# An FP32 cross-attention kernel: a third form made on GpSimd, another order of work in the steady batches, and new durations in the planner

## The chip, the cores and the metric

The kernel runs on one core of one Trainium2 chip. The metric is the device time of one execution in microseconds (us), taken as the median of several runs. TensorE is called PE in the profile, its weight loads PEld, VectorE DVE, ScalarE ACT, GpSimd POOL and SyncE SP; a `q` behind a name means the engine's queue, which issues transfers.

## The reference, cut to what matters

There are 32 batches; x and y (`ctx_2048`) are 32 x 256 x 1024 in float32, the weights 256 x 256.

```python
B, C, N = (8, 256, 1024)          # B is 32 in the inputs
x_q = jnp.einsum('oc,bcn->bno', w_qk, y)
x_k = jnp.einsum('oc,bcn->bon', w_qk, x)
x_v = jnp.einsum('oc,bcn->bon', w_v, x) + b_v[None, :, None]
energy = jnp.einsum('bnc,bcm->bnm', x_q, x_k)
attention = jax.nn.softmax(energy, axis=-1)
attention = attention / (1e-07 + attention.sum(axis=1, keepdims=True))
x_r = jnp.einsum('bcn,bnm->bcm', x_v, attention)
x_r = jax.nn.relu(jnp.einsum('oc,bcn->bon', w_t, x - x_r) + b_t[None, :, None])
return x + x_r
```

## The kernel before, in words

**Forms.** The operands of PE are tiles of type float32r. Each operand is split into three forms: for x, y and ef these are HIGH (the value written as float32r), REST (the value less HIGH) and LOW (HIGH/4096 + REST); gf, uf and the weights have variants of them. A product is a sum of three float32r products, taken in the order HIGH, REST, LOW. The two query and key weight matrices are multiplied together once, in the set-up (`gw`), and w_t is multiplied into w_v (`vw`), so each batch has five kinds of product, all of 128 x 128 weights by 512 columns:

- `k0`, `k1` (`keys`): gw times x gives gf, a pair of PSUM banks for each, 12 matmuls for each. ACT and DVE then make gf's three forms from the banks.
- `V0`, `V1` (or `v0`, `v1`; `values`): x times vw, 12 matmuls each. DVE transposes blocks into the tile `turned`, SP writes it to DRAM in four transfers (`blocks<-turned`) and reads it back: the first half into `yr` (`yr<-blocks`), the second into `turned`. From there ACT and POOL make the three forms `uf`.
- `W0`, `W1` (`straight`): x times tw, 12 matmuls each, which ACT copies with a bias into `xe`.
- `E0` to `E7` (`energy`): 128 rows of y times gf, 12 matmuls, two banks of 512 columns (h0, then h1). Then the softmax of these rows: DVE takes the minimum, ACT the exponential with its sum, DVE the reciprocal; for each half DVE adds the scaled row to `acc`, ACT makes HIGH of `ef`, DVE makes REST; ACT makes LOW and POOL adds REST to LOW. The pair of banks is free again after the last REST.
- `A0` to `A7` (`attention`): uf times ef, 12 matmuls into pairs 2 and 3, where all eight add up.

Then `S` (`sums`) sums `acc` down the columns on DVE, and `O` (`finish`) scales the attention result, adds `xe`, applies relu, adds x (`xo`) and stores. `Y2` and `Y3` (`load_y`) load the two halves of the next batch's y, `X` (`load_x`) the next batch's x.

**PSUM.** Of four pairs of banks, pairs 0 and 1 alternate among `E`, `k` and `v`; a unit marked `^` takes pair 3 or 2 in turn, while attention does not hold them.

**Buffers.** There is one raw buffer `yr` (128 x 1024 float32, 512 KB) for y's halves, which the read-back `yr<-blocks` also uses; two buffers `yf` of y's forms, one for each half of the rows (E0 to E3 read the first, E4 to E7 the second); four buffers `ef`.

**Order.** The strings SET_UP, FIRST (batch 0), STEADY (batches 1 to 29), BEFORE (batch 30) and LAST (batch 31) list units; PE does them exactly in that order. All the rest is ordered by a planner (`Plan`): each unit adds its operations with an assumed engine duration (`busy`), a time until others see the result (`lag`, for transfers the landing), and the names it reads and writes. The planner works out due times and runs a list schedule over the whole program; what comes out of it is each engine's fixed instruction order, and ties go to the operation that was listed first. The engines then run their queues strictly in order. SP issues loads, read-backs and stores; POOL issues the adding transfers.

**y's forms before.** In `load_y`, SP loads `yr`, ACT copies it to HIGH. ACT then writes -HIGH into the third form, and a transfer that POOL issues adds y itself from DRAM onto it (`yf<-in_ctx_dram`), which gives REST. ACT writes HIGH/4096 into LOW and a second adding transfer (`yf<-yf`) adds REST. In the set-up alone, y's first half is cut in two pieces of 256 columns, and the first piece's REST and LOW are made on POOL by `tensor_tensor`; the second piece is read by E2 and E3.

Of the kernel before, what the change touches and what calls it, by code (L numbers as in the profile page):

```python
# [16 lines left out]
class Plan:  # L17
# [146 lines left out]

SET_UP = (
    "z z x0 z z z z G H fH00 x1 fH01 T fR01 fL00 y fR00 fL01 Q fR11 fH10 fR10 fL10 b fH11 fL11"
)
# [1 line left out]
    "V0^ W0^ W1^ E0 E1^ V1^ E2 E3 A0 A1 E4 X Y2 E5 A2 A3 E6 E7 A4 Y3 A5 v0 k0 S A6 A7 k1 O"  # L171
)
STEADY = (
    "W0^ E0^ E1 E2 W1^ V1^ E3 Y2 A0 E4 A1 E5 A2 X E6 A3 E7 Y3 S A4 A5 v0 k1 A6 A7 k0 O"
)
BEFORE = (
    "V1^ E0 W0^ E1 W1^ X E2 A0 E3 A1 E4 A2 E5 A3 E6 E7 Y2 A4 Y3 A5 v0 k0 k1 A6 S A7 O"
# [7 lines left out]
def kernel(  # L185
# [55 lines left out]
        plan.add("pe", count * (columns / 2400 + 1 / 400), 0.163, reads, writes, trace)  # L241

    def on_act(columns, reads, writes, trace, more=0.0):
        plan.add("act", columns / 1200 + 0.1 + more, 0.09, reads, writes, trace)

    def on_dve(columns, reads, writes, trace, early=0.0):
        plan.add("dve", columns / 960 + 0.16, 0.0, reads, writes, trace, early=early)

    def dve_in_sbuf(columns, reads, writes, trace):
        busy = columns / 960 + 0.07  # L250
# [3 lines left out]
        plan.add("dve", busy, 0.0, reads, writes, trace)  # L254

    def on_pool(columns, reads, writes, trace):
        busy = columns * 2.25 / 1024 + 0.12
        plan.add("pool", busy, 0.0, reads, writes, trace, port=busy)

    def by_sync(landing, reads, writes, trace, early=0.0):  # L260
        plan.add("sync", 0.4, landing, reads, writes, trace, early=early)
# [7 lines left out]
    def value(v):  # L269
        return v.bitcast(F32)  # L270
# [7 lines left out]
    def parted(v):  # L278
        return v.rearrange("p (a b) -> p a b", a=2)
# [60 lines left out]
    def load_y(q):  # L340
        b, half = divmod(q, MH)
        s = q % NY
        f, r = yf[s], yr
        from_ = y[b].rearrange("(k p) n -> p k n", p=P)[:, :, ts(half, MB)]
        by_sync(5.8 if q else 7.4, [], ["yr"], lambda: sync.dma_start(r, from_), early=0.0 if q else 10.0)
        on_act(N, ["yr"], y_names(s, HIGH), lambda: act.copy(f[:, HIGH], r))

        def pieces(which):
            at = slice(which[0] * QB, (which[-1] + 1) * QB)
            high, low, third = (f[:, j, :, at] for j in range(FORMS))  # L350
            nh, nl, nr = (y_names(s, j, which) for j in range(FORMS))
            columns = KC * QB * len(which)
            if q == 0 and which[0] == 0:
                on_pool(
                    columns, ["yr"] + nh, nr,
                    lambda: pool.tensor_tensor(third, r[:, :, at], value(high), ALU.subtract),
                )
                on_act(columns, nh, nl, lambda: act.mul(low, value(high), 1.0 / UP))
                on_pool(columns, nl + nr, nl, lambda: pool.tensor_tensor(low, value(low), value(third), ALU.add))
                return  # L360
            on_act(columns, nh, nr, lambda: act.mul(third, value(high), -1.0))
            by_pool(7.2, nr, nr, lambda: accumulate(third, from_[:, :, at]))
            on_act(columns, nh, nl, lambda: act.mul(low, value(high), 1.0 / UP))
            by_pool(5.8, nl + nr, nl, lambda: accumulate(value(low), value(third)))

        for which in ([0], [1]) if q == 0 else ([0, 1],):
            pieces(which)
# [4 lines left out]
    def load_x(b):  # L372
        for k in range(KC):

            def of(k=k):
                raw = [f"xr{k}{h}" for h in range(MH)]
                by_sync(5.0, ["yr"] if b == 1 else [], raw, lambda: sync.dma_start(xr[:, k], x[b, ts(k, P)]))
                on_act(N, raw, x_names(HIGH, k), lambda: act.copy(parted(xf[:, HIGH, k]), in_turn(xr[:, k])))
                on_pool(
                    N, raw + x_names(HIGH, k), x_names(REST, k),  # L380
                    lambda: pool.tensor_tensor(
                        parted(xf[:, REST, k]), in_turn(xr[:, k]), parted(value(xf[:, HIGH, k])), ALU.subtract
                    ),
                )
                on_act(
                    N, x_names(HIGH, k), x_names(LOW, k),
                    lambda: act.mul(xf[:, LOW, k], value(xf[:, HIGH, k]), 1.0 / UP),
                )
                by_pool(
                    8.2, x_names(LOW, k) + x_names(REST, k), x_names(LOW, k),  # L390
                    lambda: accumulate(value(xf[:, LOW, k]), value(xf[:, REST, k])),
                )

            of()
# [41 lines left out]
    def values(b, q, j_pair):  # L436

        both, at, u = pair(j_pair), in_pair(j_pair), uf[q]
        for i in range(KC):
            for j in ORDER:  # L440

                def of(i=i, j=j):
                    for k in range(KC):
                        matmul(
                            both[:, i], vw[:, j, k, ts(i, P)], woven(xf[:, j, k], q),
                            j == ORDER[0] and k == 0, j == ORDER[-1] and k == KC - 1,
                        )

                on_pe(KC, MB, [f"vw{j}{k}" for k in range(KC)] + [f"xf{j}{k}{q}" for k in range(KC)], [at[i]], of)
        on_dve(  # L450
            N, at, ["turned"],
            lambda: dve.transpose(
                turned.rearrange("p (a t i r) -> p i t a r", a=NG, t=HT, i=KC),
                both.rearrange("p i (t a r) -> p i t a r", t=HT, a=NG),
            ),
        )
        names = [f"uf{q}{j}" for j in range(FORMS)]

        def out_of():
            for g in range(NG):  # L460
                sync.dma_start(
                    blocks.rearrange("(a r) (g s) -> r g a s", a=NG, g=NG)[:, g],
                    turned[ts(g, G32)].rearrange("p (a s) -> p a s", a=NG),
                )

        plan.add("sync", 2.4, 3.0 if b else 5.0, ["turned"], ["blocks"], out_of)
        back, name = (turned, "turned") if q else (flat(yr), "yr")
        by_sync(4.5, ["blocks"], [name], lambda: sync.dma_start(back, blocks))

        def natural(v):  # L470
            return v.rearrange("p (t g s) -> p g t s", t=HT, g=NG)

        raw = back.rearrange("p (g t s) -> p g t s", t=HT, g=NG)
        high, low, rest = (natural(u[:, j]) for j in range(FORMS))
        on_act(N, [name], [names[HIGH]], lambda: act.copy(high, raw))
        on_pool(
            N, [name, names[HIGH]], [names[LOW]],
            lambda: pool.tensor_tensor(low, raw, value(high), ALU.subtract),
        )
        on_act(N, [names[LOW]], [names[LOW]], lambda: act.mul(u[:, LOW], value(u[:, LOW]), UP))  # L480
        on_pool(
            N, [name, names[LOW]], [names[REST]],
            lambda: pool.tensor_tensor(rest, raw, value(low), ALU.subtract),
        )
# [9 lines left out]
    def energy(b, n, jp):  # L494
# [6 lines left out]
        for j, h in steps:  # L501
# [13 lines left out]
        on_dve(N, at, [nm[0]], lambda: dve.tensor_reduce(low, p, AX.X, ALU.min))  # L515
        on_act(
            N, at + [nm[0]], at + [nm[1]],
            lambda: act.activation(p, p, AF.Exp, bias=low, scale=-1.0, accum_out=rs), more=0.193,
        )
        dve_small(0.18, [nm[1]], [nm[2]], lambda: dve.reciprocal(ri, rs))  # L520

        def halves(h):
            ph, a, turns = both[:, h], acc[:, ts(h, MB)], in_turn(both[:, h])
            to = {j: parted_half(f[:, j], h) for j in (HIGH, REST)}
            high, rest = names[HIGH][h], names[REST][h]
            if n == 0:
                on_dve(MB, [at[h], nm[2]], [f"acc{h}"], lambda: dve.tensor_scalar(a, ph, ri, None, ALU.mult))
            else:
                on_dve(
                    MB, [at[h], nm[2], f"acc{h}"], [f"acc{h}"],  # L530
                    lambda: dve.scalar_tensor_tensor(a, ph, ri, a, ALU.mult, ALU.add),
                )
            on_act(MB, [at[h], nm[2]], [high], lambda: act.mul(to[HIGH], turns, ri))
            on_dve(
                MB, [at[h], nm[2], high], [rest],
                lambda: dve.scalar_tensor_tensor(
                    to[REST], turns, ri, value(to[HIGH]), ALU.mult, ALU.subtract
                ),
            )

        for h in range(MH):
            halves(h)
        on_act(N, names[HIGH], names[LOW], lambda: act.mul(f[:, LOW], value(f[:, HIGH]), 1.0 / UP))
        on_pool(
            N, names[LOW] + names[REST], names[LOW],
# [229 lines left out]
    def first_x(k):  # L775
        for h in range(MH):

            def of(h=h):
                at = ts(h, MB)
                high, low, rest = (parted_half(xf[:, j, k], h) for j in range(FORMS))  # L780
                raw, (nh, nl, nr) = in_turn(xr[:, k, at]), (x_names(j, k, (h,)) for j in range(FORMS))
                on_act(MB, [f"xr{k}{h}"], nh, lambda: act.copy(high, raw))
                dve_in_sbuf(MB, [f"xr{k}{h}"] + nh, nr, lambda: dve.tensor_tensor(rest, raw, value(high), ALU.subtract))
                dve_in_sbuf(
                    MB, nh + nr, nl,
# [181 lines left out]
```

## Time and profile before

| | |
|---|---|
| median of 3 runs | 1881.93 us (1878.26 to 1883.33) |
| the profiled execution, its own time | 1882.61 us |
| its span, first to last instruction | 1880.7 us |
| mean granted TensorE clock | 0.998 |
| busy, of the span | PE 1855.6 us (99%), PEld 1597.4, POOL 1541.4 (82%), DVE 1493.0 (79%), ACT 1484.8 (79%) |
| DMA | 301.88 MB, of which 99.10 MB from POOL's queue |

How to read it: matmuls overlap one another, so PE's busy time counts their modelled lengths; the rate at which they start is what tells the time. A row of the timeline has its start, its length, the engine, the operation, the tile written and those read, the count of instructions that were merged, and in brackets the idle time before it with what ended that. A row of the windows gives, for a stretch of time, the busy time and the count of each engine, then the granted clock (PEclk), the DMA engines' busy share and their rate.

### The profile page before, as it was taken

The page shows a single profiled execution, that of the slowest core. Times are in us where ns is not written, and L with a number is a line of the kernel's source. Part 1 is how long each engine was busy: PE and PEld are TensorE (multiplying, and loading weights), DVE is VectorE, ACT ScalarE, POOL GpSimd, SP SyncE. Part 2 cuts the span into 40 slices and gives each one's busy share as a digit, 9 for nine tenths or more (in the row PEclk, how much of TensorE's full clock was granted, in tenths as well). Part 3 has the DMA queues.
Part 4 walks back from the last instruction along what each step waited for, and adds up shares of the span by engine and source line. Part 5 has one row for each costly group of instructions (what it writes and reads, how often), then busy time and mean ns, then how long its engine had stood idle before and what let it go on. Part 6 is the DMA issues. An engine that isn't in the chain of part 4 may idle for free.

```text
span 1880.7 us, 24352 instructions
## 1 busy us (share of the span) xinstructions
PE 1855.6 (99%) x8494; PEld 1597.4 (85%) x8494; DVE 1493.0 (79%) x2106; ACT 1484.8 (79%) x1936; POOL 1541.4 (82%) x773
## 2 busy tenths in 40 slices
PE   8999999999999999999999999999999999999998
PEld 7888888888888888888888888888888888888887
DVE  6787777887778878878777787777887877877878
ACT  6788777897777987778877789777797777887775
POOL 4788888888788888788888888888888788888777
PEclk9999999999999999999999999999999999999999
DMA  6666766667667667666676666666767666667652
GB/s 187 137 154 169 178 157 157 162 163 178 160 154 170 154 183 173 152 153 162 167 180 157 157 160 165 175 160 152 174 152 184 169 154 151 170 165 177 150 119 79
DMA packets 128651, 301.88 MB, mean 161 GB/s; under 512 B 12688, under 2 KB 47120, under 8 KB 128528
## 3 DMA queue, kind: packets, MB, share of 16 engines
q1 hardware_dynamic: 92272, 200.45, 34.4%
q0 software_dynamic: 35680, 99.10, 31.0%
q8 instruction: 66, 1.08, 0.2%
q10 hardware_dynamic: 576, 0.79, 0.1%
q14 instruction: 57, 0.47, 0.1%
HBM read 167.38 MB, written 67.11 MB: 125 GB/s over the span
## 4 chain that ended last, share of the span: by engine, by line
PE 33%; ACT 28%; DVE 14%; DMA 11%; issue 8%; POOL 4%; SPq 1%; DVEq 0%; POOLq 0%; ACTq 0%
PE banks L231 33%; ACT ef L231 10%; DMA blocks<-turned 6%; ACT banks L231 5%; DVE ef L231 5%; ACT xf L231 5%; DMA yr<-blocks 4%; DVE acc L231 4%; ACT xe L231 3%; ACT uf L231 3%; POOL ef L231 2%; DVE small L231 2%; ACT z L231 1%; SPq L231 1%; DVE parts L231 1%
## 5 line engine op out<-in xcount | busy, mean ns | idle before, releaser
L231 PE MATMUL banks<-gf,yf 128*128 128x512 f32 x3072 | 705.5, 381 | 8.5 <-DMA yf<-yf 2.8
L231 POOL TENSOR_TENSOR ef<-ef 128x1024 fp32r<-128x1024 f32 x256 | 640.5, 2516 | 79.8 <-DVE acc L231 35.4
L231 PE MATMUL banks<-ef,uf 128*128 128x512 f32 x3072 | 694.7, 379 | 1.1 <-POOL ef L231 0.6
L231 PEld LDWEIGHTS banks<-gf,yf 128*128 128x128 f32 x3072 | 576.2, 189 | 107.5 <-DVE ef L231 24.9
L231 PEld LDWEIGHTS banks<-ef,uf 128*128 128x128 f32 x3072 | 580.2, 189 | 85.1 <-POOL ef L231 1.4
L231 DVE TENSOR_REDUCE small<-banks 128x1 f32<-128x1024 f32 x256 | 312.5, 1221 | 174.1 <-PE banks L231 174.1
L231 DVE SCALAR_TENSOR_TENSOR ef<-banks,small,ef 128x512 fp32r<-128x512 f32 x512 | 366.5, 742 | 48.5 <-ACT ef L231 47.6
L231 ACT ACTIVATE ef<-banks,small 128x512 fp32r<-128x512 f32 x512 | 335.5, 706 | 4.1 <-DVE acc L231 0.6
L231 DVE SCALAR_TENSOR_TENSOR acc<-banks,small,acc 128x512 f32<-128x512 f32 x448 | 319.6, 743 | 5.7
L231 ACT ACTIVATE banks<-banks,small 128x1024 f32<-128x1024 f32 x256 | 281.8, 1101 | 23.2 <-DVE small L231 23.0
L231 ACT ACTIVATE ef<-ef 128x1024 fp32r<-128x1024 f32 x256 | 276.7, 1081 | 1.2
L231 ACT ACTIVATE gf<-banks 128x1024 fp32r<-128x1024 f32 x64 | 65.4, 1023 | 261.7 <-PE banks L231 259.8
L231 POOL TENSOR_TENSOR z<-z,xe 128x1024 f32<-128x1024 f32 (+1 forms) x64 | 149.1, 2345 | 68.2 <-DVE z L231 65.7
L231 POOL TENSOR_TENSOR uf<-yr,uf 128x1024 fp32r<-128x1024 f32 x64 | 152.2, 2377 | 57.4 <-ACT uf L231 57.1
L231 PE MATMUL banks<-xf,vw 128*128 128x512 f32 x768 | 183.4, 383 | 7.5 <-DVE ef L231 6.7
L231 PE MATMUL banks<-xf,gw 128*128 128x512 f32 x768 | 177.3, 380 | 1.1 <-DVE xf L231 0.7
L231 PE MATMUL banks<-xf,tw 128*128 128x512 f32 x774 | 176.5, 378 | 0.9 <-DVE banks L231 0.9
L231 PEld LDWEIGHTS banks<-xf,vw 128*128 128x128 f32 x768 | 142.6, 189 | 38.2 <-DVE ef L231 19.2
L231 PEld LDWEIGHTS banks<-xf,gw 128*128 128x128 f32 x768 | 144.7, 189 | 23.5 <-ACT acc L231 1.1
L231 PEld LDWEIGHTS banks<-xf,tw 128*128 128x128 f32 x774 | 145.4, 189 | 22.1 <-DVE banks L231 1.3
L231 POOL TENSOR_TENSOR uf<-turned,uf 128x1024 fp32r<-128x1024 f32 x64 | 154.9, 2420 | 8.5 <-ACT uf L231 6.2
L231 POOL TENSOR_TENSOR xf<-xr,xf 128x1024 fp32r<-128x1024 f32 x62 | 149.3, 2429 | 1.0 <-ACT xf L231 1.0
(68 smaller groups left out, 1633.8 us busy)
## 6 DMA issues: line engine op xcount, KB each, us to landing
yr<-in_ctx_dram SPq DMA_DIRECT2D x64, 512.0 KB, 4.3
blocks<-turned SPq DMA_DIRECT2D x256, 128.0 KB, 3.2
yf<-in_ctx_dram POOLq DMA_DIRECT2D x63, 512.0 KB, 6.1
yf<-yf POOLq DMA_DIRECT2D x63, 512.0 KB, 7.4
xo<-in_x_dram SPq DMA_DIRECT2D x62, 512.0 KB, 4.4
xr<-in_x_dram SPq DMA_DIRECT2D x62, 512.0 KB, 4.8
xf<-xf POOLq DMA_DIRECT2D x62, 512.0 KB, 6.7
out_dram<-z SPq DMA_DIRECT2D x62, 512.0 KB, 4.1
```

Of the source, the lines that this page charges most:

```text
L231: self.last = getattr(self.engine, name)(*args, **kwargs)
```

## The change

1. In `load_y`, the third form is made by POOL as a difference, yr - HIGH, in one `tensor_tensor`. ACT's multiplication by -1 and the adding transfer from DRAM are gone. `yr` is then read by POOL too.
2. STEADY has a new order. On PE it differs in one place: `E3 A0 E4 A1 E5 A2 E6 A3 E7` becomes `E3 A0 A1 E4 E5 A2 A3 E6 E7`. The units without PE work `Y2`, `X`, `S` and `O` stand elsewhere in the list.
3. The planner's durations change: ACT, DVE and POOL operations, ACT's copies of x (+0.47 us, +0.26 in the set-up), the exponential, and the landings of transfers. They alter no instruction, only the order in which instructions are queued.
4. The softmax's pieces are listed as both column sums, both HIGH, both REST, with the switches SUMS, HIGHS, RESTS all at 2 (two halves each, as before).

```diff
+SUMS, HIGHS, RESTS = 2, 2, 2
+LAND_Y, LAND_X, LAND_BLOCKS, LAND_BACK, LAND_LOW = 4.8, 4.5, 2, 5.2, 5
...
 STEADY = (
-    "W0^ E0^ E1 E2 W1^ V1^ E3 Y2 A0 E4 A1 E5 A2 X E6 A3 E7 Y3 S A4 A5 v0 k1 A6 A7 k0 O"
+    "W0^ E0^ E1 E2 W1^ V1^ E3 A0 A1 E4 E5 A2 A3 E6 Y2 X E7 Y3 A4 A5 v0 k1 A6 A7 S O k0"
 )
...
     def on_act(columns, reads, writes, trace, more=0.0):
-        plan.add("act", columns / 1200 + 0.1 + more, 0.09, reads, writes, trace)
+        plan.add("act", columns / 1200 + 0.13 + more, 0.1, reads, writes, trace)
     def on_dve(columns, reads, writes, trace, early=0.0):
-        plan.add("dve", columns / 960 + 0.16, 0.0, reads, writes, trace, early=early)
+        busy = columns / 960 + (0.08 if columns > MB else 0.13)
+        plan.add("dve", busy, 0.08, reads, writes, trace, early=early)
...
     def on_pool(columns, reads, writes, trace):
-        busy = columns * 2.25 / 1024 + 0.12
-        plan.add("pool", busy, 0.0, reads, writes, trace, port=busy)
+        busy = columns * 2.25 / 1024 + 0.07
+        plan.add("pool", busy, 0.08, reads, writes, trace, port=busy)
...
-        by_sync(5.8 if q else 7.4, [], ["yr"], lambda: sync.dma_start(r, from_), early=0.0 if q else 10.0)
+        by_sync(LAND_Y if q else 7.4, [], ["yr"], lambda: sync.dma_start(r, from_), early=0.0 if q else 10.0)
...
-            on_act(columns, nh, nr, lambda: act.mul(third, value(high), -1.0))
-            by_pool(7.2, nr, nr, lambda: accumulate(third, from_[:, :, at]))
+            on_pool(
+                columns, ["yr"] + nh, nr,
+                lambda: pool.tensor_tensor(third, r[:, :, at], value(high), ALU.subtract),
+            )
             on_act(columns, nh, nl, lambda: act.mul(low, value(high), 1.0 / UP))
-            by_pool(5.8, nl + nr, nl, lambda: accumulate(value(low), value(third)))
+            by_pool(LAND_LOW, nl + nr, nl, lambda: accumulate(value(low), value(third)))
...
-                by_sync(5.0, ["yr"] if b == 1 else [], raw, lambda: sync.dma_start(xr[:, k], x[b, ts(k, P)]))
-                on_act(N, raw, x_names(HIGH, k), lambda: act.copy(parted(xf[:, HIGH, k]), in_turn(xr[:, k])))
+                by_sync(LAND_X, ["yr"] if b == 1 else [], raw, lambda: sync.dma_start(xr[:, k], x[b, ts(k, P)]))
+                on_act(
+                    N, raw, x_names(HIGH, k), lambda: act.copy(parted(xf[:, HIGH, k]), in_turn(xr[:, k])), more=0.47
+                )
...
-                    8.2, x_names(LOW, k) + x_names(REST, k), x_names(LOW, k),
+                    LAND_LOW, x_names(LOW, k) + x_names(REST, k), x_names(LOW, k),
...
-        plan.add("sync", 2.4, 3.0 if b else 5.0, ["turned"], ["blocks"], out_of)
+        plan.add("sync", 1.75, LAND_BLOCKS if b else 5.0, ["turned"], ["blocks"], out_of)
-        by_sync(4.5, ["blocks"], [name], lambda: sync.dma_start(back, blocks))
+        by_sync(LAND_BACK, ["blocks"], [name], lambda: sync.dma_start(back, blocks))
...
-            lambda: act.activation(p, p, AF.Exp, bias=low, scale=-1.0, accum_out=rs), more=0.193,
+            lambda: act.activation(p, p, AF.Exp, bias=low, scale=-1.0, accum_out=rs), more=0.1,
...
-        for h in range(MH):
-            halves(h)
+        each, whole = [[h] for h in range(MH)], [list(range(MH))]
+        for make, pieces in ((column_sums, SUMS), (high_form, HIGHS), (rest_form, RESTS)):
+            for hs in each if pieces == MH else whole:
+                make(hs)
```

More of the change, by code (lines that the diff above doesn't have):

```diff
@@ L517, in energy, with part @@
             N, at + [nm[0]], at + [nm[1]],
-            lambda: act.activation(p, p, AF.Exp, bias=low, scale=-1.0, accum_out=rs), more=0.193,
+            lambda: act.activation(p, p, AF.Exp, bias=low, scale=-1.0, accum_out=rs), more=0.1,
         )
         dve_small(0.18, [nm[1]], [nm[2]], lambda: dve.reciprocal(ri, rs))
[L522 to L525, printed above, removed]
+        def part(t, hs):
+            return t[:, hs[0] * MB : (hs[-1] + 1) * MB]
@@ L526, in halves, with column_sums @@
+        def column_sums(hs):
+            ph, a = part(p, hs), part(acc, hs)
+            banks_, sums_ = [at[h] for h in hs], [f"acc{h}" for h in hs]
             if n == 0:
-                on_dve(MB, [at[h], nm[2]], [f"acc{h}"], lambda: dve.tensor_scalar(a, ph, ri, None, ALU.mult))
+                on_dve(
+                    MB * len(hs), banks_ + [nm[2]], sums_,
+                    lambda: dve.tensor_scalar(a, ph, ri, None, ALU.mult),
+                )
             else:
                 on_dve(
-                    MB, [at[h], nm[2], f"acc{h}"], [f"acc{h}"],
+                    MB * len(hs), banks_ + [nm[2]] + sums_, sums_,
@@ L531, in halves, with turned_to, high_form @@
                     lambda: dve.scalar_tensor_tensor(a, ph, ri, a, ALU.mult, ALU.add),
                 )
-            on_act(MB, [at[h], nm[2]], [high], lambda: act.mul(to[HIGH], turns, ri))
+        def turned_to(j, hs):
+            return parted(f[:, j])[:, :, hs[0] * MB // 2 : (hs[-1] + 1) * MB // 2]
+        def high_form(hs):
+            turns = in_turn(part(p, hs))
+            on_act(
+                MB * len(hs), [at[h] for h in hs] + [nm[2]], [names[HIGH][h] for h in hs],
+                lambda: act.mul(turned_to(HIGH, hs), turns, ri),
+            )
@@ L534, in halves, with rest_form @@
+        def rest_form(hs):
+            turns = in_turn(part(p, hs))
             on_dve(
-                MB, [at[h], nm[2], high], [rest],
+                MB * len(hs), [at[h] for h in hs] + [nm[2]] + [names[HIGH][h] for h in hs],
+                [names[REST][h] for h in hs],
                 lambda: dve.scalar_tensor_tensor(
-                    to[REST], turns, ri, value(to[HIGH]), ALU.mult, ALU.subtract
+                    turned_to(REST, hs), turns, ri, value(turned_to(HIGH, hs)), ALU.mult, ALU.subtract
@@ L781, in of @@
                 raw, (nh, nl, nr) = in_turn(xr[:, k, at]), (x_names(j, k, (h,)) for j in range(FORMS))
-                on_act(MB, [f"xr{k}{h}"], nh, lambda: act.copy(high, raw))
+                on_act(MB, [f"xr{k}{h}"], nh, lambda: act.copy(high, raw), more=0.26)
                 dve_in_sbuf(MB, [f"xr{k}{h}"] + nh, nr, lambda: dve.tensor_tensor(rest, raw, value(high), ALU.subtract))
```

## The prediction

> **What bounds the kernel now.** I read the page's line of busy times first, then the windows, the waits, and the timeline at the places where PE waits.
>
> ```profile
> PE 1855.6 (99%) x8494; PEld 1597.4 (85%) x8494; DVE 1493.0 (79%) x2106; ACT 1484.8 (79%) x1936; POOL 1541.4 (82%) x773
> 147.48:1767.24 1619.76, 1610.76 (x7394) 1390.09 (x7392) 1294.52 (x1821) 1295.64 (x1680) 1353.45 (x673) 1.00 0.68 164
> 957.79:1015.35 57.56, 57.43 (x266) 49.66 (x265) 46.18 (x66) 46.34 (x60) 48.36 (x25) 1.00 0.68 162
> 947.43 5.34 PE L231 MATMUL banks<-ef,uf 128*128 128x512 f32 x24
> 952.61 2.75 PE L231 MATMUL banks<-xf,gw 128*128 128x512 f32 x12
> ```
>
> PE is the bound: 24 matmuls take 952.61 - 947.43 = 5.18 us, 0.2158 us each. A batch has 264, so 56.98 us. The third row spans 28 steady batches from E0 to E0: 1619.76/28 = 57.85 us each. All that order and waits can give there is 0.87 us a batch; one of the best batches (fourth row) has 0.58. These waits are the subject, and few rows hold them:
>
> ```profile
> PEld banks L231 <- DVE ef L231: 44.8, 100, 1.6
> ACT gf L231 <- PE banks L231: 259.8, 60, 6.7
> POOL yf L231 <- DMA yf<-in_ctx_dram: 69.8, 29, 7.3
> ```
>
> PE's loads wait almost only for DVE's last REST of ef, which frees a pair of banks. ACT's 259.8 us of idleness lie at the two `k` units; between those, ACT is full. In batch 16:
>
> ```profile
> 968.15 2.92 PE L231 MATMUL banks<-xf,vw 128*128 128x512 f32 x12
> 973.24 3.02 ACT L231 CAST xf<-xr 128x1024 fp32r<-128x1024 f32 x2
> 976.10 3.15 PE L231 MATMUL banks<-gf,yf 128*128 128x512 f32 x12
> 976.88 0.75 DVE L231 SCALAR_TENSOR_TENSOR ef<-banks,small,ef 128x512 fp32r<-128x512 f32 x1 [1.03 <-ACT ef L231]
> 977.68 1.16 PEld L231 LDWEIGHTS banks<-gf,yf 128*128 128x128 f32 x6 [0.53 <-DVE ef L231]
> 979.09 2.75 PE L231 MATMUL banks<-ef,uf 128*128 128x512 f32 x12
> 1729.58 0.51 PEld L231 LDWEIGHTS banks<-gf,yf 128*128 128x128 f32 x3 [0.53 <-DVE ef L231]
> ```
>
> E4 (976.10) takes 979.09 - 976.10 = 2.99 us instead of 2.59: its second half waits for E2's last REST (976.88), which itself waited for ACT's HIGH of ef, and ACT was copying x for 3.02 us (973.24), where the plan counts 2 x 0.95. The same 0.53 us stands in the last of these batches (1729.58): I take 0.40 us for every batch. The rest of the 0.87 I put down to V1 (968.15, 2.92 us long instead of 2.75), which waits for E0's pair and whose wait differs from batch to batch.
>
> **Part 1, y's third form.** Rows for the head, and the prices:
>
> ```profile
> 18.38 1.33 POOL L231 DMA_DIRECT2D yf<-in_ctx_dram  x1
> 25.61 1.21 POOL L231 DMA_DIRECT2D yf<-in_ctx_dram  x1 [4.58 <-ACT yf L231]
> 26.25 0.34 SPq L231 DMA_DIRECT2D yr<-blocks  x1
> 26.37 1.69 POOL L231 DMA_DIRECT2D yf<-yf  x1
> 33.41 1.03 PE L231 MATMUL banks<-gf,yf 128*128 128x512 f32 x4
> 34.59 1.05 ACT L231 CAST uf<-yr 128x1024 fp32r<-128x1024 f32 x1
> 37.27 6.27 PE L231 MATMUL banks<-gf,yf 128*128 128x512 f32 x20 [2.84 <-DMA yf<-yf]
> 39.79 2.36 POOL L231 TENSOR_TENSOR uf<-yr,uf 128x1024 fp32r<-128x1024 f32 x1 [1.17 <-ACT uf L231]
> 43.38 4.91 PE L231 MATMUL banks<-ef,uf 128*128 128x512 f32 x22
> 37.20:41.40 4.20, 4.13 (x11) 3.33 (x12) 2.82 (x4) 2.70 (x3) 3.03 (x2) 0.59 1.00 214
> L231 POOL DMA_DIRECT2D yf<-in_ctx_dram x64 | 78.6, 1234 | 30.3 <-DVE ef L231 25.7 <-ACT yf L231 4.6
> L231 ACT ACTIVATE yf<-yf 128x1024 fp32r<-128x1024 f32 x126 | 140.1, 1112 | 0.0
> 995.91 1.21 POOL L231 DMA_DIRECT2D yf<-in_ctx_dram  x1
> 998.39 2.38 POOL L231 TENSOR_TENSOR ef<-ef 128x1024 fp32r<-128x1024 f32 x1 [1.27 <-DVE acc L231]
> ```
>
> In batch 0, E2 stops for LOW of y's second piece: POOL issues its adding transfer only at 26.37, behind the transfer of 25.61, and it lands as PE goes on at 37.27. After the change the difference (half of 2.38, 1.2 us) stands where POOL issued the transfer at 18.38, and LOW's transfer can go by about 22; even with the old 10.9 us to land it is there before 33.41. PE loses there 37.27 - (33.41 + 4 x 0.2158) = 3.00 us, and then 43.38 - 37.27 - 20 x 0.2158 = 1.79 us, because the granted clock behind the wait is 0.59 (window 37.20:41.40): 4.8 us in all. [...]
>
> What is late next is A0: its third-form products would start at 43.38 - 4.8 + 4 x 0.2158 = 39.5, and need uf's last difference, which ended at 42.15. That chain hangs on `yr<-blocks`, issued at 26.25, cast at 34.59 beside the transfers that vanish or move. If it lands as late as now, 2.65 us come back, if 2.65 us earlier, nothing; a landing earlier by the missing transfer alone is likely, so I take 1.0. Head: -3.8 us (bounds -4.8 and -2.1).
>
> In each steady batch ACT loses 2 x 1.11 = 2.2 us out of 46.34. POOL gains 2 x (2.38 - 1.23) = 2.3 us on 48.36 in 57.56, and loses its wait for the transfer, 69.8/32 = 2.2 us. In the one stretch where POOL hardly rests, the row of 995.91 has 1.27 us idle behind it, and the difference needs 1.15 more: it fits. If that cover were gone, the ef sums behind it would be late, and `A`'s last third with them (a rival). `yr` is now free only after POOL's difference. Its next user is SP's queue, with x's and the output's transfers behind it:
>
> ```profile
> 940.58 1.09 ACT L231 CAST yf<-yr 128x1024 fp32r<-128x1024 f32 x1
> 955.57 0.34 SPq L231 DMA_DIRECT2D yr<-blocks  x1
> ```
>
> From the end of the cast, 941.67, to the read-back are 13.9 us; the difference behind one ef sum takes 2 x 2.38 = 4.8. Hidden, 0 us; without cover it would be 2.4 us a batch on uf's chain. With 64 fewer transfers of 512 KB, landings can only shorten. Price of all this: 0.
>
> **Part 2, the order.** In PE's order only A1 and E4 change places, likewise A3 and E6. E4 comes one unit (2.59 us) later, so E2's REST, 0.53 us late, is early by 2.06: -0.40 x 29 = -11.6 us. What gets nearer: E6's banks are now wanted by `v0` after E7 A4 A5 instead of A3 E7 A4 A5, 7.77 us instead of 10.36; A3, A4 and A6 have 12.95 us from their E instead of 15.54. And E4, E5 and then E6, E7 arrive in pairs: E4's banks have the same 7.77 us, but E5's work on DVE and ACT starts 2.59 us into them, not 5.18. The nearest rows are those of the batches that already run in pairs:
>
> ```profile
> 54.19 5.34 PE L231 MATMUL banks<-ef,uf 128*128 128x512 f32 x24
> 60.61 5.85 PE L231 MATMUL banks<-gf,yf 128*128 128x512 f32 x24 [1.08 <-DVE ef L231]
> 52.79 2.03 ACT L231 ACTIVATE xf<-xf 128x1024 fp32r<-128x1024 f32 x2
> 1853.34 5.34 PE L231 MATMUL banks<-gf,yf 128*128 128x512 f32 x24
> ```
>
> In batch 0, E6 starts 60.61 - 54.19 - 5.18 = 1.24 us late, with ACT busy on x's forms when E4's exponential was due. In the last batch, which loads neither x nor y, E6 (1853.34) has no idle time before it. So the paired order costs between 0 and 1.24 us a batch, by what ACT does beside it. Steady batches have x's forms like batch 0, but 1.1 us less of y's on ACT per half. I take 0.1 us a batch, +2.9 us, near the lower end, because of part 3; the other end is a rival.
>
> The moves of Y2, X, S and O have no PE work and change no dependency, only ties: 0.
>
> **Part 3, the durations.** No instruction changes. Where the plan errs now, the trace says by how much: x's copies 3.02 us for 1.9 planned. The plan learns that, so batch 0's E6 may lose part of its 1.24 us; I take -0.6 (bounds 0 and -1.2). V1's waits, (0.87 - 0.58) x 29 = 8.4 us, come from the batch's start, whose unit order is unchanged: 0, with bounds -8.4 and +8.4. The landing of adding transfers is now planned as 1.2 + 5 = 6.2 us from issue:
>
> ```profile
> xf<-xf POOLq DMA_DIRECT2D x62, 512.0 KB, 6.7
> 987.78 0.95 POOL L231 DMA_DIRECT2D xf<-xf  x1
> 999.81 0.38 PE L231 MATMUL banks<-xf,vw 128*128 128x512 f32 x1
> ```
>
> That is 0.5 us too short for x's, so it may be queued too late; but it has 12.0 us until `v0` (999.81) and needs 6.7, so 5.3 us cover it: 0 us. Without cover it would be 0.5 us a batch. Part 4 keeps the same instructions and dependencies: 0.
>
> **The sum**: -3.8 - 11.6 + 2.9 - 0.6 = -13.1 us. The profiled execution took 1882.61 us, 0.68 above the median of 1881.93; so 1868.8, say 1869 us.
>
> **The rivals.** (a) Slower: the pairs queue up at E6 in every steady batch as in batch 0. 1.24 x 29 = +36.0, against -11.6 - 3.8: +20.6, 1902 us. For it: ACT is as full there, and x's forms lie there too. Against it: the last batch, and ACT's 2.2 us of relief. It decides from (5.6 + 15.4)/29 = 0.72 us a batch. (b) No change: the 0.40 us only moves, to `v0` or E5, since a fixed queue order always has a tightest place: 1882 - 3.8 = 1878 us. For it: all of 0.53 us is one just-in-time release. (c) POOL becomes the late one and the ef sums miss `A`. The nearest price is in batch 0:
>
> ```profile
> 66.29 1.89 PE L231 MATMUL banks<-ef,uf 128*128 128x512 f32 x8
> 68.34 3.72 PE L231 MATMUL banks<-ef,uf 128*128 128x512 f32 x16 [0.15 <-POOL ef L231]
> ```
>
> 68.34 - 66.29 - 8 x 0.2158 = 0.32 us; by 29 it is +9.3, in all 1876 us. Against it: 7 us of POOL's 57.56 stay free. [...]
>
> **How the numbers follow.** Likeliest case 0.60, its own range 1855 to 1877 (V1's bounds and the head's). (a) 0.16, also in part (a wait between 0.72 and 1.24); (b) 0.17; (c) 0.07. A measurement here tells about 0.3%, 5.6 us, from no change. Faster: 0.60 and a little of (c), less the likeliest's upper edge: 0.62. Same: (b), the rest of (c): 0.21. Slower: (a), 0.17. The range for 8 in 10 leaves out the upper half of (a) and the lowest tail: 1853 to 1889.
>
> **What would show it.** No `yf<-in_ctx_dram` row and 64 POOL differences `yf<-yr,yf`; no wait of 2.8 us for `yf<-yf` in batch 0 and a clock of 1.00 there; E4 without a wait in the middle; a steady batch of about 57.5 us. The prediction is wrong if PE's loads wait for DVE's ef at E6, E7, `v0` or `k1` by more than 0.7 us a batch, or for POOL's ef in `A`.

## The result, and the profile after

The changed kernel takes 1848.96 us (1848.35 to 1849.36, 4 runs) against 1880.1 us (1877.52 to 1883.33, 4 runs): ratio 0.9833, 95% interval 0.9815 to 0.9851. That is 31 us faster, where 13 were forecast: the sign was right, the forecast is less than half of the change, and 1849 lies below the range of 1853 to 1889.

First the page of the changed kernel, the lines of the busy times and of the chain of waits, and then the chain of the kernel before, which the prediction does not use:

```profile
span 1847.3 us, 24243 instructions
PE 1835.2 (99%) x8494; PEld 1603.6 (87%) x8494; DVE 1481.5 (80%) x2106; ACT 1446.2 (78%) x1872; POOL 1608.9 (87%) x773
...
PE 97%; DVE 1%; issue 0%; DMA 0%; POOL 0%; ACT 0%; POOLq 0%; SPq 0%; DVEq 0%; ACTq 0%
```
```profile
PE 33%; ACT 28%; DVE 14%; DMA 11%; issue 8%; POOL 4%; SPq 1%; DVEq 0%; POOLq 0%; ACTq 0%
PE banks L231 33%; ACT ef L231 10%; DMA blocks<-turned 6%; ACT banks L231 5%; DVE ef L231 5%; ACT xf L231 5%; DMA yr<-blocks 4%; DVE acc L231 4%; ACT xe L231 3%; ACT uf L231 3%; POOL ef L231 2%; DVE small L231 2%; ACT z L231 1%; SPq L231 1%; DVE parts L231 1%
```

Both kernels have PE at 99%. The chain tells them apart: before, what ended last led through PE for only a third of the span and went through ACT, DVE and the values' way through DRAM (`blocks<-turned`, `yr<-blocks`); after, it is PE nearly throughout. The windows of the changed kernel, from E0 of batch 1 to E0 of batch 30, one steady batch, and a stretch of batch 0; then its waits:

```profile
83.99:1736.41 1652.42, 1652.42 (x7657) 1446.23 (x7656) 1330.12 (x1886) 1307.85 (x1683) 1463.53 (x697) 1.00 0.57 148
938.69:995.67 56.98, 56.98 (x265) 49.90 (x264) 45.92 (x66) 45.19 (x58) 50.47 (x25) 1.00 0.59 152
41.70:45.00 3.30, 3.30 (x8) 2.67 (x9) 3.30 (x6) 3.30 (x5) 3.30 (x2) 0.50 0.61 158
```
```profile
PEld banks L233 <- DVE ef L233: 3.6, 4, 1.1
ACT uf L233 <- DMA yr<-blocks: 32.4, 15, 5.3
```

1652.42/29 = 56.98 us: every steady batch runs at the rate of its 264 matmuls, with no wait at all (44.8 us of PE's loads waiting for DVE's ef became 3.6). The same 29 batches took 1767.24 - 87.43 = 1679.8 us before. So 27.4 of the 33.4 us between the two spans come from there; 1.2 from the time until E0 of batch 0, 2.2 from batch 0, 0.7 from batch 30 and 1.9 from the last.

### The profile page after: what moved, and what is told of

Read it like the earlier page. It is cut to its first block, busy times and chain, and to the rows that moved or that the text cites. A ratio compares the mean times of both kernels' runs of the same rounds, so it can differ in the third digit from the quotient of the medians.

```text
span 1847.3 us, 24243 instructions
## 1 busy us (share of the span) xinstructions
PE 1835.2 (99%) x8494; PEld 1603.6 (87%) x8494; DVE 1481.5 (80%) x2106; ACT 1446.2 (78%) x1872; POOL 1608.9 (87%) x773
## 4 chain that ended last, share of the span: by engine, by line
PE 97%; DVE 1%; issue 0%; DMA 0%; POOL 0%; ACT 0%; POOLq 0%; SPq 0%; DVEq 0%; ACTq 0%
PE banks L233 97%; DMA z<-in_L_xattn_w_t_dram 0%; DVE small L233 0%; DVE acc L233 0%; DVE ef L233 0%; DVE xf L233 0%; POOL ef L233 0%; POOL uf L233 0%; ACT banks L233 0%; ACT ef L233 0%; DVE parts L233 0%; POOLq L989 0%; DVE turned L233 0%; POOL z L233 0%; SPq L233 0%
## 5 line engine op out<-in xcount | busy, mean ns | idle before, releaser
L233 PE MATMUL banks<-ef,uf 128*128 128x512 f32 x3072 | 686.7, 380 | 2.8 <-POOL uf L233 1.5
L233 PE MATMUL banks<-gf,yf 128*128 128x512 f32 x3072 | 684.9, 379 | 0.6 <-DVE ef L233 0.6
L233 POOL TENSOR_TENSOR ef<-ef 128x1024 fp32r<-128x1024 f32 x256 | 622.0, 2443 | 36.3 <-ACT ef L233 27.1
L233 DVE SCALAR_TENSOR_TENSOR ef<-banks,small,ef 128x512 fp32r<-128x512 f32 x512 | 370.9, 743 | 57.1 <-ACT ef L233 57.0
L233 ACT ACTIVATE ef<-banks,small 128x512 fp32r<-128x512 f32 x512 | 341.5, 691 | 13.0 <-DVE acc L233 9.7
L233 DVE SCALAR_TENSOR_TENSOR acc<-banks,small,acc 128x512 f32<-128x512 f32 x448 | 324.3, 745 | 5.2
L233 ACT ACTIVATE ef<-ef 128x1024 fp32r<-128x1024 f32 x256 | 269.7, 1066 | 1.8
L233 POOL TENSOR_TENSOR yf<-yr,yf 128x1024 fp32r<-128x1024 f32 (+1 forms) x65 | 153.8, 2367 | 41.2 <-ACT yf L233 41.2
L233 PE MATMUL banks<-xf,vw 128*128 128x512 f32 x768 | 176.2, 379 | 0.0
L233 POOL TENSOR_TENSOR uf<-turned,uf 128x1024 fp32r<-128x1024 f32 x64 | 159.9, 2498 | 12.3 <-ACT uf L233 12.3
```

What stands on the lines that cost most here:

```text
L233: self.last = getattr(self.engine, name)(*args, **kwargs)
```

## Experiments

Three theories were set against each other at the start: D, the planner's durations carry the gain; O, the order of units; F, the form, by ACT's relief and GpSimd's free queue. A fourth came later: L, that the gain comes from the transfer's being gone, because while it is there it delays other landings and stands in a queue. H is the part of L that speaks of ACT's queue. Every time below is the median of a kernel's runs, with the ratio to the kernel before in the same session, in which that kernel took 1880.1 to 1883.8 us.

### Each part alone

Three kernels are the one before with one hunk of the diff: the STEADY string (order), the third form in `load_y` (form), or all durations and landings (durations). The listing of the softmax's pieces (SUMS, HIGHS, RESTS) was left out of all of these: with the other three parts in, it leaves every engine's instruction order as it is.

```diff
 e1  -    "W0^ E0^ E1 E2 W1^ V1^ E3 Y2 A0 E4 A1 E5 A2 X E6 A3 E7 Y3 S A4 A5 v0 k1 A6 A7 k0 O"
     +    "W0^ E0^ E1 E2 W1^ V1^ E3 A0 A1 E4 E5 A2 A3 E6 Y2 X E7 Y3 A4 A5 v0 k1 A6 A7 S O k0"
 e2  -  plan.add("act", columns / 1200 + 0.1 + more, 0.09, reads, writes, trace)
     +  plan.add("act", columns / 1200 + 0.13 + more, 0.1, reads, writes, trace)
...
 e3  -  by_pool(7.2, nr, nr, lambda: accumulate(third, from_[:, :, at]))
     +  lambda: pool.tensor_tensor(third, r[:, :, at], value(high), ALU.subtract),
```

> The new order of units in the steady batches alone; y's third form and the planner's durations as before. Theory D (the durations carry the gain: with true durations the planner queues each release before PE needs it): PE's waits in a steady batch stay near the 0.87 us of before, only moved; 1875 to 1890 us. Theory O (the order carries it): E4's wait of 0.40 us goes, V1's too, a batch of 57.0 to 57.3 us, 1855 to 1870 us. Theory F (ACT's relief and POOL's free queue carry it): about as before, 1876 to 1886 us.

> The planner's new durations alone; order of units and y's third form as before. Theory D: most of the waits of the steady batches go, a batch within 0.3 us of 56.98, 1850 to 1862 us. Theory O: E4's wait of 0.40 us a batch stays, since E4 still comes right after A0; 1868 to 1885 us. Theory F: about as before, 1875 to 1885 us.

> y's third form as a difference on GpSimd alone; order and durations as before. Theory F: V1's wait goes and the wait of 3.0 us in batch 0 with the half clock behind it, 1860 to 1872 us. Theories D and O: the head alone, 1875 to 1880 us, with a steady batch of about 57.8 us.

The order alone: 1873.02 us, ratio 0.9962 (0.9948 to 0.9976). The durations alone: 1902.45 us, 1.0119 (1.0091 to 1.0147), slower. The form alone: 1872.14 us, 0.9955 (0.9940 to 0.9969). In e3 the steady batches are alike at 57.70 us, with small fixed waits for DVE's ef in each. None of the three is half of the gain, and they do not add up: -7.8 + 21.7 - 8.7 = +5 us, against the -31 measured for all. None of these times lies in a range that D, O or F gave for it (e3's misses F's by 0.14 us), and theory D in its plain form fell at once. In e1 the waits of E4 and V1 for DVE are gone from nearly all steady batches, but E0 now waits in some of them for y's second adding transfer, whose result it needs early, since E0 takes LOW before REST (a row of its waits):

```profile
PE banks L231 <- DMA yf<-yf: 14.8, 13, 3.4
```

### Two parts together

> Order and durations of the changed kernel, y's third form by ACT and the adding transfer as before. Theories D and O: steady batches at 56.98 us, only the head as before: 1850 to 1855 us. Theory F: steady batches still wait for a release, because ACT has 2.2 us more a batch: 57.3 us or more, 1860 us or more.

> New order and y's third form as a difference; the planner's durations as before. The order alone left one wait in the steady batches: E0's LOW products for y's second adding transfer, 0 to 2.1 us a batch. Theory P (order and form suffice: the order gives the banks time, the form takes the two chained transfers out of E0's way): steady batches within 0.1 us of 56.98, 1850 to 1856 us. Theory Q (the true durations are needed as well): some release stays late in each batch, 0.2 us or more, 1858 to 1868 us.

> y's third form and the durations of the changed kernel, order of units as before (E4 right behind A0). Durations alone made the old order slower by waits for E0's and E2's pairs and for ef sums of GpSimd. Theory P: the old order is what is too tight, and no schedule of the other engines frees it: 57.5 us or more a batch, 1868 to 1885 us. Theory Q: with ACT's relief the true durations do free it: under 57.2 us a batch, 1850 to 1860 us.

| parts in the kernel | median us | a steady batch, us | late starts of PE, us in 29 batches |
|---|---|---|---|
| none | 1880.1 | 57.92 | V1 15.0, E4 11.5 |
| order | 1873.02 | 57.66 | E0 15.6, V1 2.1, E4 1.6 |
| durations | 1902.45 | 58.64 | V1 23.1, E3 12.2, A3 and A4 9.7 |
| form | 1872.14 | 57.71 | E5 12.8, V1 7.7 |
| order, durations | 1856.05 | 57.20 | V1 6.2 |
| form, order | 1868.65 | 57.53 | E4 15.0, E6 1.0 |
| form, durations | 1851.99 | 57.02 | E4 0.6 |
| all | 1848.96 | 56.98 | none |

The third column is the time from E0 of batch 1 to E0 of batch 30, divided by 29, in the profiled run; in e1 that is the fastest of its runs (1870.04 us), in e2 the slowest (1909.36). The last column adds up, from the traces, by how much the starts of PE's matmuls lie further apart than 0.2158 us, and names the units with the largest sums. In e4 most steady batches run at 56.98 us and two of the first wait 2.7 to 3.1 us for DVE's ef, which lies between its two expectations. Theory P failed for e5 and for e6: form and order leave 0.55 us a batch, while form and durations with the old order, E4 right behind A0, leave almost nothing (ratio 0.9838, 0.9821 to 0.9856). So the swap of A1 and E4, to which the prediction gave 11.6 us, is worth 0.04 us a batch once the other two are there. The durations, harmful alone, are worth 20 us beside the form, 17 beside the order, and 20 beside both (18 by the ratios). With form and order, but without them, E4 waits for DVE's ef in every batch (two rows of e5's waits in the steady batches):

```profile
PEld banks L231 <- DVE ef L231: 19.8, 29, 1.1
PE banks L231 <- DVE ef L231: 8.2, 29, 0.7
```

And e4 has the transfer in it and still loses next to nothing after its first two batches: with the new order and the new durations the planner finds queue orders that leave the transfer room.

### What the durations are good for

> The changed kernel, but ACT still writes -HIGH into the third form before GpSimd overwrites it with the difference; the planner knows of it. So ACT has its 2.2 us a batch again and the transfer is still gone. Theory T (the form's worth lies in the missing transfer): steady batches stay at 56.98 us, 1848 to 1851 us. Theory R (it lies in ACT's relief): waits for DVE's ef come back, 0.2 us or more a batch, over 1855 us.

> The changed kernel with one kind of duration as before: the planner again counts 0.98 us and not 1.45 for ACT's copies of x (the 3.02 us that made E2's release late). Theory of the prediction (this error is what made the wait): a release behind the copies is late again, 0.1 us or more a batch, 1852 us or more. Theory P: the new order leaves E2's pair 2.59 us more, so the error is hidden, 1848 to 1851 us.

> The changed kernel with the landings and SP's issue time as the planner had them before; the durations of the engines new. If the engines' durations carry the planner's part of the gain: steady batches at 56.98 us, 1848 to 1853 us. If the landings carry it: 57.2 us or more a batch as with form and order alone, 1856 to 1869 us.

> The changed kernel, with the engines' durations in the planner as before and only the landings new. If the engines' durations are what the planner needed beside form and order: about as form and order alone, 57.4 us or more a batch, 1860 to 1870 us. If the landings would do as well: 56.98 us a batch, 1848 to 1854 us.

```diff
 e7   +  on_act(columns, nh, nr, lambda: act.mul(third, value(high), -1.0))   # ahead of the difference
 e8   -  act.copy(parted(xf[:, HIGH, k]), in_turn(xr[:, k])), more=0.47
      +  act.copy(parted(xf[:, HIGH, k]), in_turn(xr[:, k]))                  # and the set-up's 0.26
 e11  -  LAND_Y, LAND_X, LAND_BLOCKS, LAND_BACK, LAND_LOW = 4.8, 4.5, 2, 5.2, 5
      +  5.8, 5.0, 3.0, 4.5, and 5.8 or 8.2; SP's four issues 2.4 instead of 1.75
 e15     the other way: these landings new, on_act, on_dve, on_pool, the exponential and the copies as before
```

e7 1850.86, e8 1851.64, e11 1852.99, e15 1851.08 us. In e7, e8 and e15 a steady batch is 56.98 us, in e11 57.03. ACT's relief of 2.2 us a batch is worth nothing there (theory R fell); the copies' 0.47 us, the error that the prediction found in the trace, is not needed either; and either half of the new durations, engines or landings, does what both do. Only with neither is a wait of 0.55 us there (e5). No single number carries it.

### The transfer by itself

e13 and e14 keep every engine's order of the kernel before and of e2, instruction for instruction, and exchange only the adding transfer from DRAM for a GpSimd sum of the same size that does not use y. e16 keeps the order of the changed kernel and puts ACT's -HIGH and the transfer at the place of the difference; the planner still counts the difference there, and not the transfer's landing.

```diff
 e13, e14  -  by_pool(7.2, nr, nr, lambda: accumulate(third, from_[:, :, at]))
           +  by_pool(7.2, nr, nr, lambda: pool.tensor_tensor(third, value(third), value(high), ALU.add))
 e16       -  lambda: pool.tensor_tensor(third, r[:, :, at], value(high), ALU.subtract),
           +  lambda: (act.mul(third, value(high), -1.0), accumulate(third, from_[:, :, at])),
```

> The kernel before with all its queue orders kept, instruction for instruction; only the transfer that adds y from DRAM is replaced by a GpSimd sum of the same size over the third form and HIGH (the third form of y is then zero). Theory L (the transfer delays the read-back, and ACT's queue stands): the differing part of the waits, V1's, goes; E4's 0.40 us stays; a batch of 57.4 to 57.6 us, all alike; 1864 to 1874 us. Rival (only a new queue order helps): 57.8 us a batch, 1877 to 1884 us.

> The durations alone, which ran at 1902 us, with all its queue orders kept and the transfer from DRAM replaced in the same way by a GpSimd sum. Theory L (that order is good for landings as they are without the transfer): most of the loss goes, 1855 to 1875 us. Rival (the queue order itself is bad): 1890 us or more.

> The changed kernel with its queue orders kept; at the place of GpSimd's difference, ACT writes -HIGH and GpSimd issues the adding transfer from DRAM, as in the kernel before. Theory L: the read-back lands late and unevenly again, some or all steady batches wait 0.3 us or more, 1857 us or more. Rival (the new queue order has room enough for the transfer): steady batches at 56.98 us, under 1854 us.

e13: 1868.11 us, ratio 0.9935 (0.9919 to 0.9950). e14: 1871.57 us, 0.9952 (0.9937 to 0.9967), 31 us less than e2. e16: 1988.21 us, 1.0570 (1.0551 to 1.0588). The times of e13 and e14 lie in the ranges of theory L, and e16 is slower as it said, by far more than it asked; but the late read-back that it named for e16 did not come (ACT waits for it once, 7.9 us). A window over the steady batches and two of their batches in e13, and its wait of ACT:

```profile
82.88:1754.97 1672.09, 1666.68 (x7658) 1439.67 (x7657) 1339.40 (x1886) 1350.19 (x1740) 1466.77 (x697) 1.00 0.56 147
372.45:430.01 57.56, 57.43 (x265) 49.65 (x264) 46.17 (x66) 46.56 (x60) 50.57 (x25) 1.00 0.57 147
717.82:775.38 57.56, 57.43 (x265) 49.66 (x264) 46.20 (x66) 46.57 (x60) 50.60 (x25) 1.00 0.56 147
```
```profile
ACT uf L231 <- DMA yr<-blocks: 39.2, 31, 5.9
```

Batches that differed before are now mostly alike at 57.56 us; by the late starts of PE, E4's 11.5 us stay and V1's fall from 15.0 to 6.3. ACT's wait for the read-back fell from 79.2 to 39.2 us.

Which landing the transfer delays can be read from the times from issue to landing (medians; the kernel before, then e13):

```profile
blocks<-turned SPq DMA_DIRECT2D x256, 128.0 KB, 3.2
yr<-blocks SPq DMA_DIRECT2D x32, 512.0 KB, 4.2
...
blocks<-turned SPq DMA_DIRECT2D x256, 128.0 KB, 2.4
yr<-blocks SPq DMA_DIRECT2D x32, 512.0 KB, 7.0
```

It is the write ahead of the read-back. In both kernels SP issues the first of its four writes 10.56 us before the next E0 (medians over batches 2 to 28). The last of them has landed 2.40 us before E0 with the transfer and 6.74 without it, and SP issues the read-back behind that. The read-back then takes longer in e13, but is there 0.50 us after E0 and not 1.87. How that wait became PE's can be read in two batches of the kernel before (timeline rows of PE and ACT, batch 12 and then batch 14):

```profile
725.01 7.93 PE L231 MATMUL banks<-gf,yf 128*128 128x512 f32 x36
...
726.83 1.05 ACT L231 CAST uf<-yr 128x1024 fp32r<-128x1024 f32 x1 [2.24 <-DMA yr<-blocks]
...
729.74 1.08 ACT L231 ACTIVATE banks<-banks,small 128x1024 f32<-128x1024 f32 x1
735.37 2.82 PE L231 MATMUL banks<-xf,vw 128*128 128x512 f32 x11
...
840.55 7.93 PE L231 MATMUL banks<-gf,yf 128*128 128x512 f32 x36
...
843.59 1.05 ACT L231 CAST uf<-yr 128x1024 fp32r<-128x1024 f32 x1 [3.46 <-DMA yr<-blocks]
...
846.50 1.07 ACT L231 ACTIVATE banks<-banks,small 128x1024 f32<-128x1024 f32 x1
853.61 1.56 PE L231 MATMUL banks<-xf,vw 128*128 128x512 f32 x6 [0.89 <-DVE ef L231]
```

ACT stands at the cast until the read-back has landed, 1.82 us after E0's start in batch 12 and 3.04 us in batch 14. E0's exponential is queued behind it and comes 2.91 us after the cast in both. So E0's banks are free later, and V1 waits. Over batches 2 to 28 the start of that cast and the batch's excess over 56.98 us go together (correlation 0.92; in e2 0.95, where the cast lies up to 7.3 us behind E0).

In e16 it is another queue, POOL's, in batch 3 (timeline rows of POOL, ACT and PE, then the window over the steady batches):

```profile
206.32 1.22 POOL L231 DMA_DIRECT2D yf<-in_ctx_dram  x1 [0.99 <-ACT yf L231]
214.00 0.90 POOL L231 DMA_DIRECT2D yf<-yf  x1 [6.46 <-issue]
214.58 5.04 POOL L231 TENSOR_TENSOR z<-z,xe 128x1024 f32<-128x1024 f32 x2
217.32 1.07 ACT L231 ACTIVATE z<-z 128x1024 f32<-128x1024 f32 x1 [6.51 <-POOL z L231]
219.94 2.75 PE L231 MATMUL banks<-xf,tw 128*128 128x512 f32 x12
221.17 1.08 ACT L231 ACTIVATE banks<-banks,small 128x1024 f32<-128x1024 f32 x1
227.93 4.63 PE L231 MATMUL banks<-xf,vw 128*128 128x512 f32 x10 [5.23 <-DVE ef L231]
```
```profile
87.67:1875.73 1788.06, 1702.55 (x7657) 1471.02 (x7656) 1337.43 (x1886) 1356.14 (x1742) 1407.44 (x699) 0.97 0.63 155
```

POOL may not issue the second adding transfer before the first has landed. Behind it in POOL's queue stand z's sums, behind these in ACT's queue E0's exponential, and V1 pays 5.2 us. That the 6.46 us are the first transfer's landing is read from the issue times of 206.32 and 214.00 and the dependency in the code; the row itself says only "issue". Every second batch is like this one, 8.4 to 10.4 us over 56.98. Not all of that is the wait: behind it 10 matmuls take 4.63 us, where 12 take 2.75 ahead of it (219.94), and the granted clock is 0.97 in the window, 3% of 1788.06 us or about 54 us (an estimate from these two numbers). e16 and e4 have the same instructions and the same order on PE; e4, whose planner counts the transfer, takes 1856.05 us. So the 139 us by which e16 is over the changed kernel are the price of the transfer in a plan made without it, and not its price as such.

### Two attempts on what was left

> The kernel before with one number changed: the planner counts 7.5 us instead of 4.5 for the landing of the read-back of values (blocks to yr), as the trace shows the whole way through DRAM at 13.5 us from the end of the transposition to the end of the cast where the plan counts about 11.6. No instruction is added. Theory H (ACT waits at the head of its queue for the read-back, with E0's exponential queued behind the cast; that was V1's wait): ACT's wait for the read-back falls under 20 us in all, and the differing part of the steady batches' waits goes (the batches become alike within 0.1 us), 1865 to 1876 us if E4's 0.40 us stays. Rival (V1 waits because DVE and ACT are full at the start of the batch): the waits stay as they differ now, 1878 to 1884 us.

> The new durations alone, which made the kernel slower, but with the landing of the read-back at 8.7 us instead of 5.2. Theory H (the new durations are those of a kernel without the transfer from DRAM; with that transfer the read-back lands late and ACT's queue stands): most of the loss goes, 1855 to 1882 us. Rival (the loss is the old order of units, too tight for true durations): 1890 us or more.

> The changed kernel; the two loads of x for batch 1, which SP issued right behind the first read-back, must now wait for it (ACT copies one column out of yr into xr first, 0.2 us each). If A0's wait of 1.6 us in batch 0 and the half clock behind it come from that read-back landing beside 1 MB of x: the read-back lands in about 4.2 us instead of 6, and 2 to 3.4 us of batch 0 go, 1845 to 1847.5 us. If not: 1848 to 1851 us.

```diff
 e9   -  by_sync(4.5, ["blocks"], [name], lambda: sync.dma_start(back, blocks))
      +  by_sync(7.5, ["blocks"], [name], lambda: sync.dma_start(back, blocks))
 e10     the same line in e2: 5.2 -> 8.7
 e12  +  if b == 1:
      +      plan.add("act", 0.2, 0.1, ["yr"], raw, lambda: act.copy(xr[:, k, :1], flat(yr)[:, :1]))
```

e9: 1914.62 us, ratio 1.0182 (1.0162 to 1.0202). Theory H was right on the wait it named, 79.2 us down to 2.4, and the batches became alike; and wrong on the time, 39 us beyond its range, because the new schedule has other waits, the same in every batch:

```profile
PEld banks L231 <- DVE ef L231: 47.0, 128, 1.8
PEld banks L231 <- POOL uf L231: 38.0, 30, 5.2
```

e10: 1898.99 us, 1.0101 (1.0078 to 1.0124). ACT's wait falls here as well, from 101.0 us in e2 to 9.5, and most of the loss stays, as the rival said; GpSimd's ef sums are late instead (PE's loads wait 37.3 us for them, 15.9 in e2). So a larger number for this one landing repairs neither of the two schedules.

e12 was to beat the changed kernel and did not: 1848.45 us, ratio 0.9830 (0.9811 to 0.9848), not to be told from 1848.96. Batch 0 is 0.8 us shorter, but E3 now waits 2.53 us for DVE's ef in place of A0's waits, and behind that wait 11 matmuls still take 4.20 us (38.09), where the 12 ahead of it take 2.75 (32.81). No version here beats the change by more than a measurement tells.

## Why the prediction was right and wrong

**The step that failed**: two terms of the sum were put at or near 0 and carry the miss.

The first is part 3's -0.6 us for the durations ("bounds 0 and -1.2"), with 0 for V1's waits, "whose unit order is unchanged". Beside the form and the order the durations are worth 18 to 20 us (1868.65 to 1848.96), 15.9 of them in the steady batches (1668.36 to 1652.42). The bounds came from one wait of batch 0; an edit that makes a planner order a whole program anew has no row of the old trace as a bound.

The second is in part 1: "With 64 fewer transfers of 512 KB, landings can only shorten. Price of all this: 0". The prediction quoted POOL's 69.8 us of waiting for that transfer and took it as POOL's own idle time. e13 prices the transfer, with all orders of the kernel before fixed, at 13.9 us (1881.97 to 1868.11), of which 7.7 in the steady batches (1679.8 to 1672.09) and 3.4 in batch 0. Part 1 as a whole was to bring 3.8. These 13.9 us hold for that order; e4 shows that another order hides the transfer. Nor did all landings shorten: by the medians from issue to landing, `blocks<-turned` went from 3.2 to 2.4 us in the changed kernel and `yf<-yf` from 7.4 to 5.8, but `out_dram<-z` from 4.1 to 4.4, and in e13 `yr<-blocks` from 4.2 to 7.0.

**Where it looks right, it is in part luck.** Parts 1 and 2 of the sum give -12.5 us, 1869 us and a steady batch of about 57.5; e5, which has just these parts, took 1868.65 us and 57.53. But its waits are the wrong ones: V1's, which were to stay, are gone, and E4's, which were to go, stand at 15.0 us. Two errors of about the same size made the sum right.

**V1's term** was 0, with -8.4 as the bound. All of the steady waits beyond E4's went, 27.4 - 11.6 = 15.8 us: the bound left out the 0.18 us that even the best batch had, 5.2 us in 29, and batch 1, which lay outside the window it was taken from. No rival ended on the side of a larger gain, so the range had no case below 1853.

**E4's 0.40 us** went in the changed kernel, and the order alone takes nearly all of it away in e1. As a cause of the result it is not shown: e6 has next to no such wait under the old order, and e5 has it, and more, under the new one. So what E4 gains by coming one unit later the other engines' queues can take back.

**The pairs** cost 0, not 2.9 us, and rivals (a), (b) and (c) did not come: in the changed kernel E4 and E5 follow A1 without idle time, as does V1 (rows of PE, batch 16):

```profile
949.05 2.75 PE L233 MATMUL banks<-xf,vw 128*128 128x512 f32 x12
...
954.23 5.34 PE L233 MATMUL banks<-ef,uf 128*128 128x512 f32 x24
959.41 5.34 PE L233 MATMUL banks<-gf,yf 128*128 128x512 f32 x24
```

**POOL's load** came as worked out, 48.36 to 50.47 us a batch for 2.3 forecast, and its idle time covered it.

**The head** had about the right size by a changed course: E2's wait is gone, and E0 of batch 1 comes 3.4 us earlier (87.43 to 83.99; forecast 3.8). Of these, 1.2 us lie ahead of batch 0, where nothing was forecast. The clock of 1.00 that was to show did not come: it is 0.50 from 41.70 to 45.00 us. What was named as late next is late: A0, for uf's last difference, after two waits for DVE (rows of PE in batch 0):

```profile
36.86 1.56 PE L233 MATMUL banks<-gf,yf 128*128 128x512 f32 x6 [0.62 <-DVE ef L233]
...
39.31 0.92 PE L233 MATMUL banks<-ef,uf 128*128 128x512 f32 x3 [0.67 <-DVE ef L233]
41.68 0.80 PE L233 MATMUL banks<-ef,uf 128*128 128x512 f32 x1 [1.46 <-POOL uf L233]
```

**What stays open**: why the durations alone, with the transfer exchanged (e14), still leave 0.7 us a batch (at E3, A3 and A4), while a new plan with the same parts and the form (e6) leaves 0.04. Nor is it shown that truer durations are what helps: e8, e11 and e15 do as well with part of the old ones, and no run tries durations that are changed at random. Each schedule can be read afterwards; which one the planner finds for a given set of numbers was not to be foreseen from the trace.

## What to carry to other kernels

Where a bound engine's waits are small and differ from batch to batch, look for a transfer at the head of an in-order queue, and for what is queued behind it on that engine and the next; the chain of waits shows it when busy shares do not. Price a transfer that goes by the queues that wait for its landing (13.9 us in e13), not by its issue, and remember that such a price holds for one order of the queues. Where a planner re-orders everything, test its parts in pairs: three parts of -8, +22 and -9 us made -31 together, and a range for such a change must reach down to the bound engine's own rate (here 264 x 0.2158 us a batch).

## What the runs showed of the hardware

The prediction tied the half clock to the wait of 2.84 us and expected a full clock without it. e1 has a longer one at the same place, and the granted clock behind it is 1.00 (a row of PE, then windows before and behind the wait):

```profile
36.55 4.58 PE L231 MATMUL banks<-gf,yf 128*128 128x512 f32 x20 [3.39 <-DMA yf<-yf]
```
```profile
32.00:36.50 4.50, 1.16 (x6) 0.68 (x4) 4.31 (x7) 4.49 (x8) 2.62 (x2) 1.00 0.86 153
36.60:41.00 4.40, 4.40 (x21) 3.86 (x22) 2.69 (x4) 3.08 (x5) 3.79 (x3) 1.00 0.79 148
```

In the changed kernel three waits of 0.62, 0.67 and 1.46 us within 5 us were followed by a clock of 0.50 (window 41.70:45.00 above). So the length of a wait does not decide by itself. In windows around the drop: in the kernel before PE is idle for 2.84 of the 3.41 us from 34.27 to 37.68, at a clock of 1.00; the clock is 0.50 in 37.69:41.09 and 1.00 in 41.20:44.00. In the changed kernel PE is idle for 2.05 of the 3.41 us from 38.19 to 41.60, at 1.00; the clock is 0.50 in 41.61:45.01 and 1.00 in 45.10:48.00 (PE's ends are modelled, so the idle times are rough). Why the clock was 0.50 after these and 1.00 after the 3.39 us of e1 is not shown by these runs. A price of 1.8 us for the half clock should have been an "if".
